# First feed-forward's second product as seven products of quarters, and a turn in written order on four queues

## The chip, the cores and the metric

The kernel runs on one core of a Trainium2 chip. The metric is the device time of one execution in microseconds (us). A core has five instruction queues that run beside one another, each in order: TensorE (PE in the profile; its weight loads are listed apart as PEld), VectorE (DVE), ScalarE (ACT), GpSimd (POOL) and SyncE (SP), which here only issues DMA transfers. All data is float32.

## The reference

Two graph layers act on 64 graphs of 256 nodes with 256 features. The first is a pair of graph attentions followed by a feed-forward; the second is a relational attention with eight heads followed by another feed-forward. Cut to what is computed:

```python
# layer 0
h = gat(gat(x, adj, W1, a1), adj, W2, a2)        # softmax over axis 1 of masked leaky_relu scores
h = layernorm(x + h)
ff = relu(h @ w_ff1 + b_ff1) @ w_ff2 + b_ff2     # 256 -> 1024 -> 256
x = layernorm(h + ff)
# layer 1
q, k, v_r = x @ Wq, x @ Wk, x @ Wv[r]            # r = 0..3
out = sum_r (softmax(q k^T / sqrt(32)) * (adj == r)) @ v_r
x = layernorm(x + out @ Wo)
return layernorm(x + gelu(x @ W1 + b1) @ W2 + b2)
```

`adj` holds only 0 and 1, and the kernel keeps the values of r = 0 and the difference of r = 1 to it. The product that the change is about is `... @ w_ff2` of the first feed-forward: 256 nodes by 1024 hidden units by 256 features for each graph.

## The kernel before

Graphs are handled two at a time: a unit has 512 nodes (`TN`), in four blocks of 128 (`T`), and there are 32 units. After a prologue that folds weights (`folding`) and brings the first two units under way, the loop runs `turn(y_, x_, z)` for `y_` = 0 to 31, with `x_ = y_ + 1` and `z = y_ + 2`. In one turn, three units are at different depths: Y goes through layer 1 from queries to the second feed-forward, X through the first feed-forward of layer 0, and Z through both graph attentions. In the last two turns Z, then X, are missing. A unit whose last norm is still to come is held in `waiting` and is finished in the next turn.

The order of work: within a `tc.manual_schedule(engines=...)` block the named queues issue exactly in the order of the program text; the other queues are ordered by a planner that goes by the costs it assumes. The whole loop lies in such a block for TensorE and SP. A second block inside `turn` adds VectorE and ScalarE, from `masks(0)` to `early_adjacency(z)`, that is, for the attention part of the turn. Behind it VectorE and ScalarE are ordered by the planner, and `behind(...)` queues some of their instructions behind named ones. GpSimd is the planner's throughout.

Names and lines that matter here:

- `hidden_seven` (products at L837, VectorE accumulation at L849, ScalarE copies and activations at L846, L855, L880, the differences of inputs at L820) computes a hidden layer, 256 to 1024, from seven products of quarters. A step such as `6a` is one product of one half; a step `r` or `s` is an activation. Products 1, 6, 7 and 4 of a half add up in one PSUM bank, and each waits until VectorE has read the sum before it. It is called twice in a turn, for X (`first`) and for Y (`second`).
- `hidden_out` (matmuls at L902, residual add at L906) is the first feed-forward's second product in the plain form: four node blocks, eight blocks of hidden units, 256 output columns each.
- `hidden_out_seven` (sums of quarters at L915 to L918, matmuls at L923, adds at L928) is the second feed-forward's second product from seven products of quarters; a product is eight matmuls of 128 output columns. `out_pieces` hands it out product by product.
- `gat_softmax` with its scores, leaky ReLU (L738), exponential (L739) and masks with row sums (L741), and `scaled_rows` (L750); `gat_first` (`hpp`, L759) is the first graph attention's product with the values, and `second_sums` (`ygp`, L770) the second's.
- `norm` (statistics on VectorE at L787 and L788, the power on GpSimd at L789 and L790), `applied_norm` (L797 on VectorE, L800 on ScalarE) and `affine` (L805, L806 on VectorE).
- `normed_features` transposes 32x32 blocks on VectorE (L667), then moves quadrants with four GpSimd copies and twelve DMAs (L676, L684, L686). Y's features before the second hidden layer go half over SP's queue and half over ScalarE's.
- `queries_keys` (L969 on TensorE, L971 on ScalarE), `values` (L982, L984), `weighted` (scores L998, exponentials L1004), `masked` (L1009), `node_sums` (L1014), `applied` (L1024, L1027), `divided` (L1035 to L1040), `add_blocks` (L770, L773).

PSUM has six rotating banks under the tag `g` and one each for `po` and `zo`.

Of the kernel before, what the change touches and what calls it, by code (L numbers as in the profile page):

```python
# [385 lines left out]
def narrow_path(  # L386
# [214 lines left out]
    wf1s, w1s, w2s = [], [], []  # L601

    def folding():
# [5 lines left out]
        wf1s.extend(seven(wf1, "wf1"))  # L609
        yield  # L610
# [116 lines left out]
    def gat_softmax(u, l, wh, rows, c, aT):  # L727

        name = f"{u}_{l}"
        s = (work.tile([P, T, N], F32, tag="s", name=f"s{name}", bufs=1) if u > 1 else  # L730
             work.tile([P, 2 * T, N], F32, tag="e", name=f"s{name}")[:, :T])
        z = work.tile([P, T], F32, tag="z", name=f"z{name}")
        for b in range(G):
            for t in range(b * NB, (b + 1) * NB):
                nc.scalar.activation(s[:, t, :], rows[:, b * N:(b + 1) * N], AF.Identity,
                                     bias=wh[:, t, c:c + 1])
            sb = s[:, b * NB:(b + 1) * NB, :].rearrange("p t n -> p (t n)")
            nc.vector.scalar_tensor_tensor(sb, sb, ALPHA, sb, op0=ALU.mult, op1=ALU.max)  # L738
            nc.scalar.activation(sb, sb, AF.Exp)  # L739
            for t in range(b * NB, (b + 1) * NB):  # L740
                nc.vector.scalar_tensor_tensor(s[:, t, :], s[:, t, :], 1.0, aT[:, t, :],  # L741
                                               op0=ALU.mult, op1=ALU.mult,
                                               accum_out=z[:, t:t + 1])
        nc.vector.reciprocal(z, z)
        nc.gpsimd.tensor_add(lowg, lowg, z)
        return s, z

    def scaled_rows(wh, z, w):
        for t in range(T):
            mark["scaled"] = nc.scalar.activation(wh[:, t, :w], wh[:, t, :w], AF.Copy, scale=z[:, t:t + 1])  # L750
# [28 lines left out]
    def norm(u, l, y, blocks=range(T)):  # L779
        n, t0 = f"{u}_{l}_{blocks[0]}", blocks[0]  # L780
        bt = slice(t0, t0 + len(blocks))
        st = work.tile([P, T, 6], F32, tag="st", name=f"st{n}")
# [12 lines left out]
    def applied_norm(y, blocks, mv, rs, nm):  # L795
        bt = slice(blocks[0], blocks[0] + len(blocks))
        nc.vector.scalar_tensor_tensor(nm[:, bt], mv[:, bt, 0], -1.0, rs[:, bt],  # L797
                                       op0=ALU.mult, op1=ALU.mult)
        for t in blocks:
            mark["normed"] = nc.scalar.activation(y[:, t, :], y[:, t, :], AF.Identity,  # L800
                                                  bias=nm[:, t:t + 1], scale=rs[:, t:t + 1])

    def affine(y, g_, b_):

        nc.vector.tensor_mul(y, y, g_[:, None, :].to_broadcast(list(y.shape)))  # L805
        nc.vector.tensor_add(y, y, b_[:, None, :].to_broadcast(list(y.shape)))  # L806

    def hidden_seven(u, l, hT, w, bi, func, h1, tt):
# [20 lines left out]
        def out(h, o, b):  # L829

            f = o * FB // 2 + 2 * h
            return h1[:, f:f + 2, b * N:(b + 1) * N]
# [18 lines left out]
        def done(h, o, b, ps=None):  # L851
            for i in range(2):
                f = o * FB // 2 + 2 * h + i
                y = h1[:, f, b * N:(b + 1) * N]
# [3 lines left out]
        def step(name):  # L858
# [19 lines left out]
            elif n == "r":  # L878
                for f in range(2 * h, 2 * h + 2):
                    nc.scalar.activation(h1[:, f, :], h1[:, f, :], func, bias=bi[:, f:f + 1])  # L880
# [15 lines left out]
    def hidden_out_block(u, l, y, h1, wo_, t):  # L896
        b, i = divmod(t, NB)
        if i == 0:
            hidden_ps[u, l] = bank(f"yfp{l}_{u}_{b}")
        ps = hidden_ps[u, l]  # L900
        for k in range(FB):
            nc.tensor.matmul(ps[:, i * F:(i + 1) * F], h1[:, k, t * P:(t + 1) * P], wo_[:, k, :],  # L902
                             start=(k == 0), stop=(k == FB - 1))
        if i == NB - 1:
            yb = y[:, b * NB:(b + 1) * NB, :].rearrange("p t f -> p (t f)")
            nc.vector.tensor_tensor(yb, ps, yb, ALU.add)  # L906

    def hidden_out_seven(u, l, y, h1, w, s1, s2, s3, s4):


        b11, b21, b22, t1, t2, t3, t4 = w
        K2, F2 = FB // 2, F // 2
        a11, a12, a21, a22 = (h1[:, k * K2:(k + 1) * K2, b * N:(b + 1) * N]
                              for b in range(2) for k in range(2))
        nc.vector.tensor_tensor(s1, a21, a22, ALU.add)  # L915
        nc.vector.tensor_tensor(s2, s1, a11, ALU.subtract)
        nc.vector.tensor_tensor(s4, a12, s2, ALU.subtract)
        mark["quarters"] = nc.vector.tensor_tensor(s3, a11, a21, ALU.subtract)  # L918

        def product(ps, a, w_, first):  # L920
            for i in range(NB):
                for k in range(K2):
                    nc.tensor.matmul(ps[:, i * F2:(i + 1) * F2], a[:, k, i * P:(i + 1) * P], w_[:, k, :],  # L923
                                     start=first and i == 0 and k == 0, stop=True, skip_group_check=True)

        def added(b, o, ps):
            yq = y[:, b * NB:(b + 1) * NB, o * F2:(o + 1) * F2]
            nc.vector.tensor_tensor(yq, ps[:, :F].rearrange("p (i f) -> p i f", i=NB), yq, ALU.add)  # L928

        n = f"{l}_{u}"  # L930
        one = bank(f"yf1{n}")
        product(one, a11, b11, True)
        added(0, 0, one)
        yield
        two = bank(f"yf3{n}")
        product(two, s1, t1, True)
        added(1, 1, two)
        yield
        ps = bank(f"yf2{n}")
        product(ps, a12, b21, True)  # L940
        added(0, 0, ps)
        yield
        product(one, s2, t2, False)
        added(0, 1, one)
        yield
        product(two, s4, b22, False)
        added(0, 1, two)
        yield
        product(one, s3, t3, False)
        added(1, 1, one)  # L950
        yield
        product(one, a22, t4, False)
        added(1, 0, one)
        yield

    hidden_ps = {}

    def hidden_out(u, l, y, h1, wo_):
        for t in range(T):
            hidden_out_block(u, l, y, h1, wo_, t)  # L960

    def queries_keys(u, hT):
        qk = []
        for w, c, name in ((wq, bq, "q"), (wk, bk, "k")):
            d = work.tile([P, KB, TN], F32, tag=name, name=f"{name}{u}", bufs=1)
            for m in range(KB):
                ps = bank(f"{name}p{u}_{m}")
                for k in range(KB):
                    nc.tensor.matmul(ps, w[:, k, m * P:(m + 1) * P], hT[k],  # L969
                                     start=(k == 0), stop=(k == KB - 1))  # L970
                nc.scalar.activation(d[:, m, :], ps, AF.Identity, bias=c[:, m:m + 1])  # L971
            qk.append(d)
        return qk
# [56 lines left out]
    def divided(u, b, po, zo, oT):  # L1030


        rz = work.tile([P, KB * N], F32, tag="rz", name=f"rz{u}_{b}", bufs=1)
# [27 lines left out]
    def first_rows(z):  # L1061
# [80 lines left out]
    def turn(y_, x_, z):  # L1142
# [132 lines left out]
        if Z:  # L1275
            second_rows(z)
# [105 lines left out]
```

## Time and profile before

| What | us |
|---|---|
| Median of three runs | 3129.61 (3126.61 to 3130.61) |
| The profiled execution | 3128.14 |
| Its span, first to last instruction | 3126.4 |
| L902, 64 matmul records, in one turn | 13.81 |
| L923, 16 matmul records | 1.78 |
| One steady turn, 1501.50 to 1596.24 | 94.74 |

The profile is of one execution, so its rows are to be set against 3128.14 and not against the median. The page gives each engine's busy time; a steady turn is cut into stretches to see which engine is busy where, and the order in time of each engine shows what an instruction waited for. A float32 matmul of this kernel leaves two records, each with a weight load; matmuls overlap at their ends, so the time of a row of them is taken from its start to the start of the next. A wait is shown in square brackets with the engine and line that ended it. TensorE's granted clock was 0.993 on average and full in the steady turns.

```profile
L902 PE MATMUL yfp<-wf,h 128*128 128x256 f32 x2048 | 447.3, 379 | 0.0
L1009 DVE TENSOR_TENSOR ea<-e,aT 128x1024 f32<-128x1024 f32 x256 | 313.2, 1253 | 79.7 <-ACT e L1004 79.7
L849 DVE TENSOR_TENSOR h<-h1a,h 128x512 f32<-128x512 f32 x384 | 263.9, 687 | 130.8 <-PE h1a L837 93.7
L787 DVE BATCH_NORM_STATS2 st<-y 128x6 f32<-128x256 f32 x512 | 198.1, 408 | 2.4
```

These rows are four of the costliest groups of instructions: line, engine, operation, tiles and shapes, count, then busy us, mean ns of one, and the idle time before them with what ended it.

### The profile page before, as it was taken

To read this page: it belongs to the slowest core of one execution; us is meant where nothing else is said; L and a number is where in the kernel's file an instruction comes from. 1 tells how busy PE (TensorE), PEld (TensorE's weight loads), DVE (VectorE), ACT (ScalarE), POOL (GpSimd) and SP (SyncE) were. 2 spreads that over 40 slices of the span, in tenths; PEclk is the share of its full clock that TensorE was granted. 3 is DMA by queue.
4 is the path that set the end of the run, shared out by engine and by line. 5 is a ranking of instruction groups with operands and counts; after the bars stand their busy time and mean duration, and the time that the engine had idled before them with its cause. 6 is when DMAs were issued, how large, how long until landed. Compare 5 with 4: busy or idle time off the path is not lost. (4 is left out here: it accounts for less than half of the span.)

```text
span 3126.4 us, 52820 instructions
## 1 busy us (share of the span) xinstructions
PE 3067.8 (98%) x19888; PEld 2327.7 (74%) x19888; DVE 2383.2 (76%) x4600; ACT 1626.6 (52%) x3274; POOL 602.5 (19%) x826
## 2 busy tenths in 40 slices
PE   7999999999999999999999999999999999999997
PEld 6677777778777778777777777787777787777766
DVE  4577777877877777777777778778778777778776
ACT  4355545555545555545555455555455555455543
POOL 3122111121111221121221111211111211212200
PEclk8999999999999999999999999999999999999999
DMA  5011111111011211111211111210111111211000
GB/s 147 13 36 34 20 38 38 43 41 33 19 42 38 43 36 24 32 43 38 43 34 20 38 38 43 43 31 20 41 38 43 36 31 25 43 38 36 22 13 15
DMA packets 428549, 113.55 MB, mean 36 GB/s; under 512 B 364760, under 2 KB 427648, under 8 KB 428288
## 3 DMA queue, kind: packets, MB, share of 16 engines
q1 hardware_dynamic: 417952, 102.66, 15.0%
q10 hardware_dynamic: 9280, 6.39, 0.8%
q8 instruction: 160, 2.62, 0.4%
q0 software_dynamic: 1056, 1.05, 0.1%
q14 instruction: 101, 0.83, 0.1%
HBM read 57.04 MB, written 16.78 MB: 24 GB/s over the span
## 5 line engine op out<-in xcount | busy, mean ns | idle before, releaser
L902 PE MATMUL yfp<-wf,h 128*128 128x256 f32 x2048 | 447.3, 379 | 0.0
L902 PEld LDWEIGHTS yfp<-wf,h 128*128 128x128 f32 x2048 | 386.8, 190 | 51.3
L1004 ACT ACTIVATE e<-sp 128x512 f32<-128x512 f32 x512 | 264.3, 603 | 282.4 <-PE sp L998 271.7
L846 ACT COPY h<-h1b 128x512 f32<-128x512 f32 x384 | 221.2, 584 | 333.9 <-PE h1b L837 331.5
L800 ACT ACTIVATE y<-y,nm,rs 128x256 f32<-128x256 f32 x512 | 270.1, 596 | 219.7 <-DVE nm L797 215.4
L1009 DVE TENSOR_TENSOR ea<-e,aT 128x1024 f32<-128x1024 f32 x256 | 313.2, 1253 | 79.7 <-ACT e L1004 79.7
L849 DVE TENSOR_TENSOR h<-h1a,h 128x512 f32<-128x512 f32 x384 | 263.9, 687 | 130.8 <-PE h1a L837 93.7
L684 POOL COPY hT<-yt 32x256 f32<-32x256 f32 x248 | 240.3, 969 | 215.9 <-DVE yt L667 187.9
L789 POOL TENSOR_SCALAR rs<-mv 128x4 f32<-128x4 f32 (+1 forms) x130 | 55.6, 428 | 1074.6 <-DVE mv L788 1069.0
L982 PE MATMUL vp<-wv,hT 128*128 128x512 f32 x480 | 214.0, 599 | 0.0
L787 DVE BATCH_NORM_STATS2 st<-y 128x6 f32<-128x256 f32 x512 | 198.1, 408 | 2.4
L676 POOL COPY hT<-yt 32x256 f32<-32x256 f32 x120 | 111.0, 925 | 392.3 <-DVE yt L667 388.6
L982 PEld LDWEIGHTS vp<-wv,hT 128*128 128x128 f32 x480 | 88.7, 190 | 110.4 <-issue 103.2
L880 ACT ACTIVATE h<-h,cols 128x512 f32<-128x512 f32 x256 | 167.5, 718 | 1.5 <-DVE h L849 1.1
L667 DVE STREAM_TRANSPOSE yt<-y 128x256 f32<-128x256 f32 x368 | 148.1, 428 | 25.0 <-ACT y L800 20.0
L806 DVE TENSOR_TENSOR y<-y,rb 128x1024 f32<-128x1024 f32 (+1 forms) x130 | 160.1, 1232 | 2.2
L805 DVE TENSOR_TENSOR y<-y,rg 128x1024 f32<-128x1024 f32 (+1 forms) x130 | 157.2, 1210 | 5.0 <-ACT y L800 2.3
L1014 DVE TENSOR_TENSOR es<-e 128x1024 f32<-128x1024 f32 x128 | 155.6, 1216 | 0.0
L998 PE MATMUL sp<-q,k 32*128 32x256 f32 x2048 | 147.3, 400 | 6.8 <-ACT k L971 5.0
L998 PEld LDWEIGHTS sp<-q,k 32*128 32x128 f32 x2048 | 92.7, 184 | 81.5 <-issue 46.3
L971 ACT ACTIVATE q<-qp,cols 128x512 f32<-128x512 f32 x64 | 43.4, 678 | 206.8 <-PE qp L969 206.8
L1024 PE MATMUL po<-e,v 128*32 128x256 f32 x2048 | 137.0, 385 | 0.0
(236 smaller groups left out, 6248.2 us busy)
## 6 DMA issues: line engine op xcount, KB each, us to landing
hT<-yt SPq DMA_DIRECT2D x918, 32.0 KB, 2.0
y<-in_x_dram SPq DMA_DIRECT2D x32, 512.0 KB, 5.3
xq<-in_x_dram SPq DMA_DIRECT2D x240, 64.0 KB, 2.2
aq<-in_adj_dram SPq DMA_DIRECT2D x240, 64.0 KB, 2.4
out_dram<-y SPq DMA_DIRECT2D x30, 512.0 KB, 3.1
hT<-yt ACTq DMA_DIRECT2D x186, 32.0 KB, 1.9
wf<-in_L_gnn_w_ff_dram SPq DMA_DIRECT2D x2, 1024.0 KB, 7.4
w<-in_L_gnn_W_dram SPq DMA_DIRECT2D x2, 1024.0 KB
```

The source lines that it names most:

```text
L684: nc.gpsimd.tensor_copy(to, at)
L787: nc.vector.bn_stats(st[:, t, :], y[:, t, :])
L800: mark["normed"] = nc.scalar.activation(y[:, t, :], y[:, t, :], AF.Identity, bias=nm[:, t:t + 1], scale=rs[:, t:t + 1])
L806: nc.vector.tensor_add(y, y, b_[:, None, :].to_broadcast(list(y.shape)))
L846: mark["copied"] = nc.scalar.copy(out(h, o, b), pair(ps))
L849: mark["added"] = nc.vector.tensor_tensor(out(h, o, b), pair(one[h]), out(h, o, b), ALU.add)
L880: nc.scalar.activation(h1[:, f, :], h1[:, f, :], func, bias=bi[:, f:f + 1])
L902: nc.tensor.matmul(ps[:, i * F:(i + 1) * F], h1[:, k, t * P:(t + 1) * P], wo_[:, k, :], start=(k == 0), stop=(k == FB - 1))
L982: nc.tensor.matmul(ps, hT[k][:, t * P:(t + 1) * P], wvf[:, k, :], start=(k == 0), stop=(k == KB - 1))
L998: nc.tensor.matmul(ps[a][:, j * N:(j + 1) * N], k_[hp, m, j0:j0 + P], q[hp, m, b * N:(b + 1) * N], start=True, stop=True)
L1004: mark[f"exp{b * KB + m}"] = nc.scalar.activation(e[:, a, :], ps[a], AF.Exp, scale=isd)
L1009: nc.vector.tensor_tensor(ea[:, a:a + 2, :], e[:, a:a + 2, :], ab[:, None, :].to_broadcast([P, 2, NB * N]), ALU.mult)
```

## The change

The first feed-forward's second product takes the form that the second one has. `hidden_out`, `hidden_out_block` and `hidden_out_seven` go; a class `HiddenOut` serves both, with `sums`, `product` and `add` as separate calls, so that each can be put at its own place in the turn. The weight `wf2` is turned into its seven quarters in the prologue by `seven_out`, four GpSimd instructions of 128x512. The order of products becomes 1, 2, 5, 6, 3, 7, 4 in the first feed-forward and 1, 5, 2, 6, 3, 7, 4 in the second.

The block in written order now spans the whole turn, from the queries to the last product, on TensorE, SP, VectorE and ScalarE (in the last turn on TensorE and SP). The calls of `behind` inside the turn are gone. `gat_softmax` becomes a class `Softmax` whose scores, exponentials and masks are placed one by one; `affine` is split into `times` and `plus`; two of the four blocks of X's second norm are applied by GpSimd. Several steps move: the features and norm of X from the end of the turn before to this turn's head, the last norm's statistics of the waiting unit there too, Z's first softmax and `first_sums` (`hpp`) to between the new products, `sums(2)` behind `4b`. The statistics tile has one buffer, and the tile `rz` shares a buffer with the softmax's `s`.

The diff, cut to its core: unchanged lines between the parts are left out, and of the old second half of `turn`, which is printed above, the removed lines too.

```diff
+        wf2s.extend(seven_out(wf2, "wf2"))
...
+    class Softmax:
+
+        def __init__(s, u, l, wh, rows, c):
+            s.u, s.wh, s.rows, s.c = u, wh, rows, c
+            s.s = (work.tile([P, T, N], F32, tag="s", name=f"s{u}_{l}", bufs=1) if u > 1 else
+                   work.tile([P, 2 * T, N], F32, tag="e", name=f"s{u}_{l}")[:, :T])
+            s.z = work.tile([P, T], F32, tag="z", name=f"z{u}_{l}")
+
+        def block(s, b):
+            return s.s[:, b * NB:(b + 1) * NB, :].rearrange("p t n -> p (t n)")
+
+        def scores(s, b):
             for t in range(b * NB, (b + 1) * NB):
-                nc.scalar.activation(s[:, t, :], rows[:, b * N:(b + 1) * N], AF.Identity,
-                                     bias=wh[:, t, c:c + 1])
-            sb = s[:, b * NB:(b + 1) * NB, :].rearrange("p t n -> p (t n)")
-            nc.vector.scalar_tensor_tensor(sb, sb, ALPHA, sb, op0=ALU.mult, op1=ALU.max)
-            nc.scalar.activation(sb, sb, AF.Exp)
+                nc.scalar.activation(s.s[:, t, :], s.rows[:, b * N:(b + 1) * N], AF.Identity,
+                                     bias=s.wh[:, t, s.c:s.c + 1])
+            nc.vector.scalar_tensor_tensor(s.block(b), s.block(b), ALPHA, s.block(b), op0=ALU.mult, op1=ALU.max)
+
+        def exp(s, b):
+            nc.scalar.activation(s.block(b), s.block(b), AF.Exp)
+
+        def masks(s, b):
             for t in range(b * NB, (b + 1) * NB):
-                nc.vector.scalar_tensor_tensor(s[:, t, :], s[:, t, :], 1.0, aT[:, t, :],
-                                               op0=ALU.mult, op1=ALU.mult,
-                                               accum_out=z[:, t:t + 1])
-        nc.vector.reciprocal(z, z)
-        nc.gpsimd.tensor_add(lowg, lowg, z)
-        return s, z
-
-    def scaled_rows(wh, z, w):
-        for t in range(T):
-            mark["scaled"] = nc.scalar.activation(wh[:, t, :w], wh[:, t, :w], AF.Copy, scale=z[:, t:t + 1])
+                nc.vector.scalar_tensor_tensor(s.s[:, t, :], s.s[:, t, :], 1.0, g[s.u]["aT"][:, t, :],
+                                               op0=ALU.mult, op1=ALU.mult, accum_out=s.z[:, t:t + 1])
+
+        def shares(s):
+            nc.vector.reciprocal(s.z, s.z)
+            nc.gpsimd.tensor_add(lowg, lowg, s.z)
+
...
-    def applied_norm(y, blocks, mv, rs, nm):
+    def applied_norm(y, blocks, mv, rs, nm, part=None, gpsimd=False):
         bt = slice(blocks[0], blocks[0] + len(blocks))
-        nc.vector.scalar_tensor_tensor(nm[:, bt], mv[:, bt, 0], -1.0, rs[:, bt],
-                                       op0=ALU.mult, op1=ALU.mult)
-        for t in blocks:
+        if part is None or part[0] == blocks[0]:
+            nc.vector.scalar_tensor_tensor(nm[:, bt], mv[:, bt, 0], -1.0, rs[:, bt],
+                                           op0=ALU.mult, op1=ALU.mult)
+        for t in part or blocks:
+            if gpsimd:
+                nc.gpsimd.tensor_scalar(y[:, t, :], y[:, t, :], rs[:, t:t + 1], nm[:, t:t + 1],
+                                        op0=ALU.mult, op1=ALU.add)
+                continue
...
+    class HiddenOut:
+
+
+
+        def __init__(s, u, l, y, h1, w, sums):
+            K2 = FB // 2
+            s.n, s.y, s.w, s.s = f"{l}_{u}", y, w, sums
+            s.a = [h1[:, k * K2:(k + 1) * K2, b * N:(b + 1) * N] for b in range(2) for k in range(2)]
+            s.ps = {}
+
+        def sums(s, *which):
+            a11, a12, a21, a22 = s.a
+            s1, s2, s3, s4 = s.s
+            for n in which:
+                o, x_, y_, op = ((s1, a21, a22, ALU.add), (s2, s1, a11, ALU.subtract),
+                                 (s3, a11, a21, ALU.subtract), (s4, a12, s2, ALU.subtract))[n - 1]
+                mark["quarters"] = nc.vector.tensor_tensor(o, x_, y_, op)
+
+        def product(s, n):
+            b11, b21, b22, t1, t2, t3, t4 = s.w
+            K2, F2 = FB // 2, F // 2
+            if n in (1, 2, 5):
+                s.ps[n] = bank(f"yf{n}_{s.n}")
+            for old, new in ((1, 6), (6, 7), (7, 4), (5, 3)):
+                if n == new:
+                    s.ps[n] = s.ps[old]
+            a, w_ = {1: (s.a[0], b11), 2: (s.a[1], b21), 5: (s.s[0], t1), 6: (s.s[1], t2),
+                     3: (s.s[3], b22), 7: (s.s[2], t3), 4: (s.a[3], t4)}[n]
             for i in range(NB):
                 for k in range(K2):
+                    nc.tensor.matmul(s.ps[n][:, i * F2:(i + 1) * F2], a[:, k, i * P:(i + 1) * P], w_[:, k, :],
+                                     start=n in (1, 2, 5) and i == 0 and k == 0, stop=True,
+                                     skip_group_check=True)
+
+        def add(s, n):
+            b, o = {1: (0, 0), 2: (0, 0), 5: (1, 1), 6: (0, 1), 3: (0, 1), 7: (1, 1), 4: (1, 0)}[n]
+            F2 = F // 2
+            yq = s.y[:, b * NB:(b + 1) * NB, o * F2:(o + 1) * F2]
+            nc.vector.tensor_tensor(yq, s.ps[n][:, :F].rearrange("p (i f) -> p i f", i=NB), yq, ALU.add)
+
+        def __call__(s, *which):
+            for n in which:
+                s.product(n)
+                s.add(n)
+
...
+        order = tc.manual_schedule(engines={getattr(mybir.EngineType, n) for n in
+                                            ("PE", "SP", "DVE", "Activation")[:4 if X else 2]})
+        with order:
+            query(0)
+            query(1)
+            if X:
+                applied_norm(X["y"], *X.pop("n"))
+            last = norm(waiting[0][0], 3, waiting[0][1]) if waiting else None
+            key(0)
+            key(1)
+            if X:
+                X["hT"] = normed_features(x_, 0, X["y"])
+                times(X["y"], rg1)
+            scores(0)
+            if z + 1 < NG:
+                load_x(z + 1)
             masks(0)
             totals(0)
-            v = values(y_, hT, range(T))
+            v = values(y_, hT, range(0, T // 2))
+            if waiting:
+                applied_norm(waiting[0][1], *last)
+            v = values(y_, hT, range(T // 2, T), v)
             steps = first_hidden(x_) if X else None
             scores(1)
             if Z:
@@ -1206,109 +1222,147 @@
             masks(2, (2,))
             first("5b 7a 3b ra 6b")
             totals(2)
-            first("4a 7b")
+            first("4a 7b rb")
+            if X:
+                plus(X["y"], rb1)
             scores(3)
-            first("sa rb sb", 2)
+            first("sa sb", 2)
             masks(3)
             totals(3)
-            sums(2)
-            last = norm(waiting[0][0], 3, waiting[0][1]) if waiting else None
             if Z:
                 project(z, range(0, T // 2))
             first("4b")
+            sums(2)
             sums(3)
+            if X:
+                out = HiddenOut(x_, 0, X["y"], X["h1"], wf2s, out_sums(x_, 0))
+                out.sums(1, 2)
             shares(1)
             out_(0)
             piece()
             if Z:
                 project(z, range(T // 2, T))
+            if Z:
+                early_adjacency(z)
             out_(1)
             if Z:
-                first_rows(z)
+                first_scores(z)
+            n = norm(y_, 2, y)
+            if X:
+                out(1)
+            if Z:
+                Z["m"].scores(0)
+                Z["m"].scores(1)
+                Z["m"].exp(0)
+                Z["m"].exp(1)
+            if X:
+                out.sums(4)
+                out(2, 5)
+            applied_norm(y, *n)
+            if Z:
+                Z["m"].masks(0)
+                Z["m"].masks(1)
+                Z["m"].shares()
+                Z["m"].scaled(WH)
+            if X:
+                out(6)
+                hT = normed_features(y_, 2, y, queues=(nc.sync, nc.scalar))
+                out(3)
+                out.sums(3)
+            else:
+                piece()
+                hT = to_features(y, f"h3T{y_}")
+                hT = [h.rearrange("p (t a r) -> p t a r", t=T, r=32) for h in hT]
+                affine(y, rg3, rb3)
             if waiting:
-                applied_norm(waiting[0][1], *last)
-            normed(y_, 2, y)
+                affine(waiting[0][1], rg4, rb4)
+                stored(*waiting.pop(), slice(0, T))
+            if z + 1 < NG:
+                load_rows(z + 1)
             if Z:
-                early_adjacency(z)
+                first_sums(z, range(0, T // 2))
+            if X:
+                out(7)
+            if Z:
+                first_sums(z, range(T // 2, T))
+            if X:
+                out.product(4)
+            tt = work.tile([P, HPB, NB * N], F32, tag="e", name=f"tt{y_}_1")
+            second = hidden_seven(y_, 1, hT, w1s, b1, AF.Gelu, Y, tt.rearrange("p a n -> p (a n)"))
+            if X:
+                out.add(4)
+                n = norm(x_, 1, X["y"])
+            h1 = Y["h1"] = work.tile([P, FB, TN], F32, tag="h1", name=f"h1{y_}_1", bufs=1)
+            second("2a 1a 2b 1b")
+            for t, name in enumerate(("5a", "5b", "3a", "3b")):
+                second(name)
+                if X:
+                    applied_norm(X["y"], *n, [t], t > 1)
+                if X and t == 0:
+                    affine(y, rg3, rb3)
+            second("6a 6b ra rb 7a 7b")
+            if Z:
+                X["hT"] = normed_features(x_, 1, X["y"], natural=True)
+            second("sa sb 4a 4b")
+            if X and not Z:
+                X["hT"] = to_features(X["y"], f"h2T{x_}")
+            if y_ >= NG - 2:
+                pieces = out_pieces(y_, y, h1)
+                if X:
+                    left.append(pieces)
+                    affine(X["y"], rg2, rb2)
+                else:
+                    for _ in pieces:
+                        pass
+                return
+            second_scores(z)
+            out = HiddenOut(y_, 1, y, h1, w2s, out_sums(y_, 1))
+            out.product(1)
+            out.sums(1, 2)
+            Z["m"].scores(0)
+            out.add(1)
+            out.product(5)
+            Z["m"].scores(1)
+            Z["m"].exp(0)
+            Z["m"].exp(1)
+            out.add(5)
+            out.sums(4, 3)
+            out(2)
+            Z["m"].masks(0)
+            out(6)
+            Z["m"].masks(1)
+            Z["m"].shares()
+            Z["m"].scaled(F)
+            out(3)
+            affine(X["y"], rg2, rb2)
+            out(7)
             checked(z, Z["aq"])
+            if z + 1 < NG:
+                load_adjacency(z + 1)
+            second_sums(z)
+            Z["n"] = norm(z, 0, Z["y"])
+            out(4)
+            waiting.append((y_, y))
...
-        hidden_out(0, 0, g[0]["y"], g[0]["h1"], wf2)
+        first = HiddenOut(0, 0, g[0]["y"], g[0]["h1"], wf2s, out_sums(0, 0))
+        first.sums(1, 2, 4, 3)
+        first(1, 2, 5, 6, 3, 7, 4)
         normed(0, 1, g[0]["y"])
         second_sums(1)
+        g[1]["n"] = norm(1, 0, g[1]["y"])
```

## The prediction

> **What bounds the kernel now.** I read the page's busy rows first, then busy time by stretch of one steady turn, then the order in time on each engine in that turn (1501.5 to 1596.2 us).
>
> ```profile
> PE 3067.8 (98%) x19888; PEld 2327.7 (74%) x19888; DVE 2383.2 (76%) x4600; ACT 1626.6 (52%) x3274; POOL 602.5 (19%) x826
> ```
> ```profile
> 1582.43:1596.24 13.81, 13.81 (x66) 12.16 (x65) 11.28 (x27) 6.14 (x13) 4.74 (x6) 1.00 0.12 30
> 1596.24:1611.89 15.65, 15.65 (x73) 13.46 (x72) 11.64 (x30) 12.83 (x27) 1.48 (x3) 1.00 0.00 0
> 1517.15:1534.00 16.85, 16.66 (x133) 16.05 (x132) 13.82 (x31) 8.54 (x18) 3.91 (x5) 1.00 0.31 48
> 1534.00:1582.43 48.43, 48.27 (x351) 30.13 (x349) 37.50 (x59) 23.10 (x46) 8.26 (x11) 1.00 0.18 45
> ```
>
> The second fence's columns are stretch, its length, then busy us of PE, weight loads, DVE, ACT, POOL, the clock and DMA. The four stretches are a whole turn, taken from two neighbouring ones: the product to be replaced, the second hidden layer, the second layer's output products, and attention. They add to 94.74 us; PE is busy in 94.38, DVE in 74.25. The clock is full. So PE sets the end, and only two things count: PE work that goes, and places where PE waits for an in-order neighbour. The waits are seen only in the order in time:
>
> ```profile
> 1517.59 1.95 PE L923 MATMUL yf<-w,h 128*128 128x128 f32 x16
> 1519.37 1.95 PE L923 MATMUL yf<-w2t,eq 128*128 128x128 f32 x16
> 1521.16 1.95 PE L923 MATMUL yf<-w,h 128*128 128x128 f32 x16
> 1523.30 2.05 PE L923 MATMUL yf<-w2t,eq 128*128 128x128 f32 x16 [0.19 <-DVE y L928]
> 1525.19 3.74 PE L923 MATMUL yf<-w,eaq 128*128 128x128 f32 x32
> ...
> 1537.44 3.60 PE L969 MATMUL kp<-hT,wk 128*128 128x512 f32 x8
> 1541.20 1.15 PE L998 MATMUL sp<-q,k 32*128 32x256 f32 x16 [0.17 <-ACT k L971]
> ...
> 1582.43 13.98 PE L902 MATMUL yfp<-wf,h 128*128 128x256 f32 x64
> 1596.24 1.03 PE L837 MATMUL h1b<-hT,w 128*128 128x256 f32 x4
> ```
>
> Columns: start, duration (ends overlap the next row, so I use start to start), instruction, wait. L902 is the replaced product. L923 is the same seven-product form, already running in the second feed-forward: the nearest possible row.
>
> **The product.** L902: 64 records from 1582.43 to 1596.24, 13.81 us. The new form has 7 x 8 matmuls of two records: 112 records of 128 columns. L923 runs 16 of them in 1.785 us (1517.59 to 1519.37 to 1521.16; 32 in 3.57), so seven products take 12.50. **Gain 1.31 us a turn.** A rule speaks against this: the Trainium skill, "TensorE: Matmul & The Clock Gate", section "Back-to-back issue gap", says that in a stream of weight load and matmul pairs the spacing does not fall in proportion to the columns, about 81 ns at 128 columns where the column count alone gives 56. A record here is two such passes (111.5 ns in the row, twice 56), so 81 ns would make 112 x 162 = 18.1 us: 4.3 us a turn lost, some 130 in all. In the row the weights load beside the matmuls; I take the row.
>
> **VectorE's new load.** Four sums of 128x1024 (1.19 to 1.40 us by L915 to L918) and seven adds of 128x256 (0.40, L928) come, two adds of 128x512 (0.68, L906) go: +6.5 us a turn, 74.25 to some 81 of 94. It still fits; what matters is where, for it now runs in written order. In the stretch after the attention output, PE's order is score rows 0.44, products 1, 2, 5, 6, 3, two first-graph sums (1.74), product 7, the other two (1.74), product 4. PE reaches product 7 at 0.44 + 8.93 + 1.74 = 11.1 us after the last `yop` matmul. Product 7 needs s3, and VectorE has in front of it, by start-to-start steps of the trace:
>
> ```profile
> 1582.19 0.69 DVE L773 TENSOR_TENSOR y<-yop,y 128x512 f32<-128x512 f32 x1 [2.30 <-PE yop L770]
> ...
> 1595.09 1.42 DVE L738 SCALAR_TENSOR_TENSOR s<-s 128x512 f32<-128x512 f32 x2 [0.78 <-ACT s L735]
> 1596.42 0.42 DVE L820 TENSOR_TENSOR tt<-hT 128x256 f32<-128x256 f32 x1
> ```
>
> start 0.17, residual add 0.61, statistics 4 x 0.53 = 2.11, add 1 0.34, leaky ReLU 1.33 (above), s4 1.13, adds 2 and 5 0.68, nm 0.08, masks and reciprocal 1.47, add 6 0.34, four transposes 1.96, add 3 0.34, s3 1.34: 11.9 us. All of it is ready in time (product 5 ends at 6.0, ScalarE's normalisation at 8.7). So product 7 starts at 12.0 instead of 11.1, plus 0.1 of restart as after 1523.30 (1.89 us for 16). **Cost 1.0.** Here the second rule: "SBUF — State Buffer", "Who interferes with whom", says that VectorE with two SBUF inputs and a GpSimd op reading SBUF lock each other out for a whole instruction. s3 falls beside the four GpSimd copies of hT (0.87 each). By the lock it could wait 0.87 more, and the turn would be almost level. The trace has L918 beside such copies at 1.42 against 1.22 in the last turns without: I take 1.34, already above.
>
> After that nothing more is late: affine of the waiting turn to 14.4, add 7, product 4 from 15.5; Y's hT. Turn 30 shows transposes done at 3009.2 and hT landed at 3014.7, 5.5 later: here 10.3 + 5.5 = 15.8, and the hidden layer starts at 17.3. That margin is 1.5 us. ScalarE's six DMA issues (3.73 us) now stand before the copies of hp; the rows that read hp come 12 us later.
>
> **The hidden layer without cover.** The two groups of hpp sums leave the second hidden layer. They stood between its last products, whose accumulation waits for VectorE. With them, 1508.49 to 1517.15 is 8.66 us less 3.48 of hpp, 5.18. Turn 30 has none:
>
> ```profile
> 3022.63 1.89 PE L837 MATMUL h1a<-tt,w1s 128*128 128x256 f32 x8
> 3024.51 3.91 PE L837 MATMUL h1a<-tt,w 128*128 128x256 f32 x16
> 3028.25 1.04 PE L652 MATMUL h2T31p<-ident,y 128*128 128x128 f32 x8
> ```
>
> 5.62 us. **Cost 0.44.** The moved affine (2.3 us) ends before the first of these adds is due.
>
> **Waits that go.** In the second layer, sums 1 and 2 are followed at once by adds 1 and 5, so product 6 no longer waits: 1525.19 - 1521.16 - 3.57 = **0.46 gained**. Next late there is the row scaling before ygp, done some 0.5 us ahead by the same addition. At the turn's head, the normalisation of X now stands between q and k on ScalarE instead of after q's first half: k's first half is ready at about 7.0 and not 7.2, so of the 0.33 us (1541.20 - 1537.44 - 3.43) some **0.2 is gained**.
>
> **The rest at nothing.** The waiting turn's statistics (2.1 us) go to the head, the bias half of affine (1.14) behind the first hidden layer: VectorE idles 0.41 before L1009 there, and values need its adds only 7 us later. X's transposes end about 0.6 later, its 12 DMAs (7.55 us on SP, and load_x's eight behind them) land near 16.3; the subtractions ran at 16.1 and the products at 18.7. If that cover were gone, each 1 us late is 1 us. sums(2) moves behind 4b: the same PE work; the projection now ahead of it needs a bank that comes free with the first exponential of scores(3), 0.1 either way. Store and load_rows stand behind six hT DMAs and before twelve due 10 us later; a store that lands slowly (3.1 us) stays inside. Two of four normalisations to GpSimd: no row has this shape; by L599's 128x256 tensor_scalar 0.46 to 0.70 each, by its adds 1.0; the transposes come 4 us later, either is covered. The folding adds four GpSimd ops of 1.26 to 2.2 us at 48 us, where GpSimd idled 5.5.
>
> **Sum.** A full turn: -1.31 - 0.46 - 0.2 + 1.0 + 0.44 = -0.53; 30 of these -16. The prologue's product -1. Turn 30, without hpp and softmax, gains 1.3 and loses about as much waiting for s3. Together -17. The profiled execution took 3128.1 (span 3126.4, 1.7 around it): 3111; the median is 1.5 above: **3112**.
>
> **Rivals.** (1) The cover holds: VectorE gets to s3 by 11.1, or the hidden layer's gap closes. Without the first cost, -1.53 a turn: 3082; without both, 3068. For it: the DVE list is within 8% of fitting. Against: its steps are measured back to back. (2) VectorE becomes the bound: every us that its list of 11.9 grows goes straight onto PE before product 7, and the second layer has only 0.4 to 0.5 of slack. From 0.53 more a turn the kernel is slower; at 1.0 more (the port lock, or some 0.06 at each of 18 handed-over steps) +0.47 a turn, 3143. Against: VectorE's waits on signals already posted cost nothing visible in the trace. (3) Narrow matmuls load-bound: 3260; L923 excludes it.
>
> **Numbers.** Likeliest 0.52, own range 3098 to 3122; rival 1 0.28; rival 2 0.12; level 0.08. A difference under 0.2% (6 us) can't be told from none here: faster 0.83, same 0.09, slower 0.08. Range 3076 to 3131.
>
> **What would show it.** The yf product's first-layer records at 111 ns; a PE gap before product 7 of about 1 us naming DVE's s3; 5.6 us for the last three pairs of the second hidden layer; none before the second layer's product 6. Wrong if DVE reaches s3 earlier, if hT's DMAs gate the hidden layer, or if SP's order delays X's features.

## The result, and the profile after

| | before | after |
|---|---|---|
| Median of five runs | 3129.61 (3126.61 to 3132.10) | **3093.99** (3093.45 to 3096.72) |
| Profiled execution | 3128.14 | 3093.86 |
| Its span | 3126.4 | 3092.2 |
| Up to the first score rows of turn 0 | 159.67 | 153.97 |
| Mean of the 29 turns from there, us | 94.79 | 93.75 |
| The rest, from turn 29 on | 217.82 | 219.37 |

Times in us. The ratio is 0.989, 95% interval 0.9876 to 0.9904: 35.6 us faster. In the profiled pair 34.2 us are to be explained: 29 x 1.04 = 30.0 in the turns, 5.7 in the prologue, less 1.55 at the end. A turn is counted from one start of the first attention's score rows (`rows<-ident,xp`) to the next.

First the page: busy us (share of the span) and instructions of each engine, then rows of its list of groups.

```profile
PE 3040.4 (98%) x21424; PEld 2331.4 (75%) x21424; DVE 2582.8 (84%) x4888; ACT 1602.3 (52%) x3212; POOL 654.9 (21%) x892
...
L876 DVE TENSOR_TENSOR h<-h1a,h 128x512 f32<-128x512 f32 x384 | 262.5, 686 | 95.4 <-PE h1a L864 92.5
...
L961 DVE TENSOR_TENSOR y<-yf,y 128x256 f32<-128x256 f32 x448 | 182.2, 407 | 19.8 <-PE yf L953 19.4
```

VectorE carries 200 us more, TensorE 27 less. L876 is the hidden layers' accumulation, shown of before as L849: its own time is as it was, and the idle time before it fell from 130.8 to 95.4. L961 is the adds of both feed-forwards, 448 in all, where the kernel before had those of one (L928). TensorE is still busy in 98%, so only its work and its waits count. Next, the four stretches of a steady turn, with the columns as in the view of before: second hidden layer, the second layer's output products, attention, and the new product.

```profile
1483.77:1496.49 12.72, 12.72 (x58) 10.10 (x57) 10.16 (x22) 9.10 (x16) 4.21 (x4) 1.00 0.14 41
1496.49:1512.89 16.40, 16.40 (x133) 15.98 (x132) 15.68 (x31) 7.66 (x17) 3.94 (x5) 1.00 0.21 33
1512.89:1560.94 48.05, 48.05 (x350) 30.22 (x349) 39.51 (x62) 25.21 (x50) 5.63 (x11) 1.00 0.17 29
1560.94:1577.29 16.35, 16.25 (x130) 15.46 (x129) 15.03 (x39) 7.88 (x18) 6.03 (x7) 1.00 0.20 57
```

This turn is 93.52 us (the median is 93.53; before 94.75). VectorE is busy in 80.38 of it. PE has 0.10 us without work in the last stretch and none elsewhere, but a busy row also hides waits at a matmul's end, so the time is read from start to start. The order in time on TensorE, from the second hidden layer on:

```profile
1488.95 2.08 PE L864 MATMUL h1b<-hT,w1s 128*128 128x256 f32 x8
1490.87 1.89 PE L864 MATMUL h1a<-tt,w1s 128*128 128x256 f32 x8
...
1496.49 0.60 PE L724 MATMUL rows<-ident,hp 128*128 128x128 f32 x4
...
1500.51 1.95 PE L953 MATMUL yf<-w,h 128*128 128x128 f32 x16
1502.29 1.95 PE L953 MATMUL yf<-w2t,eq 128*128 128x128 f32 x16
...
1516.33 3.60 PE L979 MATMUL kp<-hT,wk 128*128 128x512 f32 x8
1519.85 0.50 PE L1008 MATMUL sp<-q,k 32*128 32x256 f32 x4
```

1490.87 to 1496.49, the last three pairs of products, is 5.62 us. Product 6 of the second layer (1502.29) follows product 2 in 1.78 us: its wait is gone. Keys to scores is 3.52 us (3.76 before). The same view where the new product runs:

```profile
1560.94 3.74 PE L953 MATMUL yf<-wf,h 128*128 128x128 f32 x32
1564.52 3.74 PE L953 MATMUL yf<-wf2t,eq 128*128 128x128 f32 x32
1568.09 1.95 PE L953 MATMUL yf<-wf,eaq 128*128 128x128 f32 x16
1569.88 1.91 PE L775 MATMUL hpp<-xp,s 128*128 128x258 f32 x8
1571.88 2.05 PE L953 MATMUL yf<-wf,eaq 128*128 128x128 f32 x16
1573.77 1.91 PE L775 MATMUL hpp<-xp,s 128*128 128x258 f32 x8
```

Two products in 3.58 and 3.57 us, one in 1.79: 111.6 ns a record. Product 7 starts 2.00 us after `hpp`, which takes 1.74, and itself takes 1.89. So 0.37 us are lost there. VectorE's order in time in that place, before product 7:

```profile
1568.82 1.41 DVE L668 STREAM_TRANSPOSE yt<-y 128x256 f32<-128x256 f32 x4
1570.16 0.39 DVE L961 TENSOR_TENSOR y<-yf,y 128x256 f32<-128x256 f32 x1
1570.46 1.36 DVE L939 TENSOR_TENSOR eaq<-h 128x1024 f32<-128x1024 f32 x1
1571.75 1.41 DVE L830 TENSOR_TENSOR y<-y,rg 128x1024 f32<-128x1024 f32 x1
```

The four transposes take 1.34 us (1568.82 to 1570.16) and s3 is done at 1571.8, 11.3 us after the last `yop` matmul.

### The profile page after: what moved, and what is told of

Same layout as the page of the kernel before. It is cut to its first block, busy times and chain, and to the rows that moved or that the text cites. A ratio compares the mean times of both kernels' runs of the same rounds, so it can differ in the third digit from the quotient of the medians.

```text
span 3092.2 us, 56427 instructions
## 1 busy us (share of the span) xinstructions
PE 3040.4 (98%) x21424; PEld 2331.4 (75%) x21424; DVE 2582.8 (84%) x4888; ACT 1602.3 (52%) x3212; POOL 654.9 (21%) x892
## 5 line engine op out<-in xcount | busy, mean ns | idle before, releaser
L821 ACT ACTIVATE y<-y,nm,rs 128x256 f32<-128x256 f32 x450 | 238.5, 591 | 228.4 <-DVE nm L814 224.0
L876 DVE TENSOR_TENSOR h<-h1a,h 128x512 f32<-128x512 f32 x384 | 262.5, 686 | 95.4 <-PE h1a L864 92.5
L1047 POOL TENSOR_TENSOR low<-low,rq 128x16 f32<-128x16 f32 x64 | 13.9, 216 | 1088.3 <-DVE rq L1046 1088.3
L685 POOL COPY hT<-yt 32x256 f32<-32x256 f32 x248 | 210.5, 849 | 64.3 <-DVE yt L668 56.6
L803 DVE BATCH_NORM_STATS2 st<-y 128x6 f32<-128x256 f32 x512 | 204.3, 401 | 0.3
L961 DVE TENSOR_TENSOR y<-yf,y 128x256 f32<-128x256 f32 x448 | 182.2, 407 | 19.8 <-PE yf L953 19.4
L805 POOL TENSOR_SCALAR rs<-mv 128x4 f32<-128x4 f32 (+1 forms) x130 | 30.3, 233 | 788.5 <-DVE mv L804 772.0
L833 DVE TENSOR_TENSOR y<-y,rb 128x1024 f32<-128x1024 f32 (+1 forms) x130 | 166.8, 1284 | 3.2
L677 POOL COPY hT<-yt 32x256 f32<-32x256 f32 x120 | 113.5, 946 | 166.6 <-DVE yt L668 162.8
L806 POOL TENSOR_TENSOR rs<-rs,mhalf 128x4 f32<-128x4 f32 (+1 forms) x130 | 142.6, 1097 | 7.9
L668 DVE STREAM_TRANSPOSE yt<-y 128x256 f32<-128x256 f32 x368 | 131.7, 414 | 7.5 <-ACT y L821 6.1
```

Of the source, the lines that this page charges most:

```text
L685: nc.gpsimd.tensor_copy(to, at)
L803: nc.vector.bn_stats(st[:, t, :], y[:, t, :])
L876: mark["added"] = nc.vector.tensor_tensor(out(h, o, b), pair(one[h]), out(h, o, b), ALU.add)
L961: nc.vector.tensor_tensor(yq, s.ps[n][:, :F].rearrange("p (i f) -> p i f", i=NB), yq, ALU.add)
```

## The experiments

Each was timed beside the kernel before, the last two kernels in a second session (medians of before 3130.8 and 3130.7 us, some 1.2 us above the one beside the changed kernel); intervals are 95%. Turns are of the profiled execution.

| Kernel | median us | ratio to before | mean turn | median turn |
|---|---|---|---|---|
| the changed kernel | 3093.99 | 0.9890 (0.9876 to 0.9904) | 93.75 | 93.53 |
| product in plain form | 3130.47 | 0.9999 (0.9991 to 1.0008) | 95.07 | 94.78 |
| s3 early | 3087.87 | 0.9865 (0.985 to 0.988) | 93.54 | 93.30 |
| s3 twice | 3128.53 | 0.9997 (0.9989 to 1.0006) | 94.87 | 94.86 |
| another hidden order | 3111.62 | 0.9943 (0.9929 to 0.9956) | 94.29 | 94.27 |
| s3 early, norm on GpSimd | **3075.28** | 0.9824 (0.981 to 0.9837) | 93.16 | 93.05 |
| s3 early, statistics first | 3103.13 | 0.9911 (0.9897 to 0.9924) | 94.01 | 94.00 |

**The product in plain form.** The changed kernel in its written order, with 64 records of 256 columns in place of the seven products; the folding of `wf2` goes too.

```diff
-                out = HiddenOut(x_, 0, X["y"], X["h1"], wf2s, out_sums(x_, 0))
+                out = PlainOut(x_, X["y"], X["h1"])
```

`PlainOut` computes one node block at each of the places of products 1, 5, 3 and 4, adds behind the second and the fourth, and has no sums.

> The first feed-forward's second product is put back to its plain form (64 records of 256 columns, no sums of quarters, two adds of 128x512), all else in the new written order. My theory, the product pays for itself: TensorE gets 1.31 us a turn back to do, and the 0.37 us wait before product 7 goes, so some 0.95 us a turn more, 3120 to 3124 us. Rival, the written order is what brings the gain and the product only breaks even under VectorE's new load: 3090 to 3100.

The order with the plain product in it is worth nothing, and my 7 to 11 us were wrong. The prologue's 6.6 us are there (153.03 instead of 159.67), and are given back in this execution, which took 2.6 us more than the median: the mean turn is 0.28 us longer than before (8 us in 29 turns), the end 3.6. An undisturbed turn is level (94.73 us; before 94.74): 0.45 us are gained in the second layer's output products and 0.38 in attention, 0.64 are lost in the second hidden layer and 0.18 at the product. From here to the changed kernel such a turn falls by 1.21 us: the product's own 1.31, less the wait of 0.37 before product 7, and 0.27 that this kernel loses by itself. That the mean falls by 1.32, the product's saving, is chance.

Six turns took 95.6 to 97.0 us. In the longest of them VectorE waits for the features hT of the second hidden layer:

```profile
740.98 0.43 DVE L846 TENSOR_TENSOR tt<-hT 128x256 f32<-128x256 f32 x1 [5.55 <-DMA hT<-yt]
```

TensorE's first product of that layer then waits 1.25 us, and product 3b 0.70. Part of this is the edit's own: the add behind the second node block stands in VectorE's queue for 3.35 us, ahead of the normalisation, so the transposes that feed hT start 9.8 us after the score rows and not 8.3. So this run does not measure the order free of such losses. The new product in the old order was not tried, and how much of it the old order would have let through stays open.

**s3 early.** Is the 0.37 us before product 7 the place of s3 in VectorE's queue?

```diff
+            if X:
+                out.sums(3)
             out_(1)
...
                 out(3)
-                out.sums(3)
```

> The sum s3 moves from behind VectorE's transposes to before the second attention output add, where VectorE idles 1.15 us. If the wait before product 7 is VectorE's list up to s3, it goes, 0.37 us a turn: about 3083 us, and the record gap before product 7 closes. If something else holds product 7 there (the copies of hpp, a bank), the gap stays and the time is 3094, or more because the add behind s3 is late.

6.1 us faster than the change, not 11. VectorE's order in time shows s3 in the idle time ahead of the residual add, which does not start later for it (0.20 us after the last `yop` matmul, as in the change):

```profile
1462.59 1.18 DVE L939 TENSOR_TENSOR eaq<-h 128x1024 f32<-128x1024 f32 x1
1463.81 0.69 DVE L789 TENSOR_TENSOR y<-yop,y 128x512 f32<-128x512 f32 x1
```

On TensorE `hpp` then takes 1.74 us, product 7 1.78, and nothing waits:

```profile
1472.98 1.91 PE L775 MATMUL hpp<-xp,s 128*128 128x258 f32 x8
1474.72 1.95 PE L953 MATMUL yf<-wf,eaq 128*128 128x128 f32 x16
1476.50 1.91 PE L775 MATMUL hpp<-xp,s 128*128 128x258 f32 x8
```

An undisturbed turn is now 93.16 us, the expected 0.37 less. But the mean fell by 0.22 only: turns of 93.4 to 94.9 us had become longer and more frequent. The hidden layer starts 0.37 us earlier, and the transfers that it reads do not. These turns are taken up below.

**s3 twice.** The dose: what does a microsecond more in this queue cost?

```diff
-                out.sums(3)
+                out.sums(3, 3)
```

> s3 is computed twice in a row at its place, so VectorE's list before product 7 grows by one sum of 128x1024, 1.2 to 1.4 us a turn, and nothing else. If TensorE waits for that list, nearly all of it goes onto the time: product 7 waits some 1.6 us instead of 0.37, 3128 to 3136 us, no faster than before the change. If the turn has slack behind it, less than 10 us.

34.5 us. TensorE's order in time:

```profile
1586.76 1.91 PE L775 MATMUL hpp<-xp,s 128*128 128x258 f32 x8
1590.09 2.05 PE L953 MATMUL yf<-wf,eaq 128*128 128x128 f32 x16 [1.43 <-DVE eaq L939]
```

The second s3 takes 1.36 us and the undisturbed turn grew by 1.33: the slope is 1 from the start, so there was no slack left in the changed kernel before product 7. And all turns but two took the same 94.85 to 94.87: with the longer wait at product 7, VectorE no longer waits for the transfers behind it.

**The long turns.** In the changed kernel 11 of 29 turns took 0.2 to 1.1 us more than 93.52. One of them in order of time, first VectorE, then ScalarE, then TensorE:

```profile
732.96 0.43 DVE L847 TENSOR_TENSOR tt<-hT 128x256 f32<-128x256 f32 x1 [2.18 <-DMA hT<-yt]
...
738.55 0.16 DVE L814 SCALAR_TENSOR_TENSOR nm<-mv,rs 128x4 f32<-128x4 f32 x1 [0.39 <-POOL rs L806]
```

```profile
738.75 0.60 ACT L821 ACTIVATE y<-y,nm,rs 128x256 f32<-128x256 f32 x1 [0.40 <-DVE nm L814]
739.26 0.56 ACT L873 COPY h<-h1b 128x512 f32<-128x512 f32 x1
```

```profile
738.43 1.10 PE L864 MATMUL h1b<-hT,w1s 128*128 128x256 f32 x4
739.88 1.13 PE L864 MATMUL h1b<-hT,w1s 128*128 128x256 f32 x4 [0.34 <-ACT h L873]
```

The transfers of hT landed late (the six on SP's queue 3.6 us after issue instead of the usual 1.9). VectorE's four subtractions wait for them; behind these in VectorE's queue stand the statistics of X's norm, behind these GpSimd's power, then nm. ScalarE waits for nm with X's normalisation (738.75), and the copy that product 3b needs stands behind that (739.26). TensorE's second half of that row waits for the copy. The first products of the layer, which read hT themselves, were in time. The other long turns fit: in all 11 the subtractions begin 16.1 to 16.8 us after the score rows, in the 18 others 15.2 to 16.0. Three kernels try this chain.

**Another hidden order**, tried on the change itself, moves products 5a and 5b forward, so that there is more room before 3b:

```diff
-            second("2a 1a 2b 1b")
-            for t, name in enumerate(("5a", "5b", "3a", "3b")):
+            second("2a 1a 5a 2b 1b 5b")
+            for t, name in enumerate(("3a", "6a", "3b", "6b")):
...
-            second("6a 6b ra rb 7a 7b")
+            second("ra rb 7a 7b")
```

> The second hidden layer's products go 2a 1a 5a 2b 1b 5b 3a 6a 3b 6b 7a 7b 4a 4b, so that two products instead of one stand between 5 and 3 and between 6a and 7a. My theory, these waits are latencies of VectorE's add and of ScalarE's copy between products of one bank: the 0.11 us before 3b (0.4 more in every third or fourth turn) and some 0.15 of the 0.44 of the last three pairs go, about 0.45 us a turn, near 3080. Rival, they are a cost of VectorE's total load and move elsewhere: 3090 to 3096.

A miss: 17.6 us slower than the change. The long turns are gone (none above 94.46), and the hidden layer takes 12.69 us where it took 12.72, so the 0.26 us hoped for inside it did not come either. Instead a new wait stands in every turn, on TensorE in the second layer's output products:

```profile
1502.63 0.60 PE L724 MATMUL rows<-ident,hp 128*128 128x128 f32 x4
...
1505.55 2.02 PE L953 MATMUL yf<-w2t,eq 128*128 128x128 f32 x16 [0.53 <-DVE eq L939]
```

ScalarE's last copy comes 8.1 us after the hidden layer's start instead of 7.3. Behind it stand the load of the gelu table (1.28 us) and the activations that the first sum reads, and product 5 starts 2.92 us after the score rows instead of 2.23. I had looked at TensorE's waits in this layer and not at what else stood behind the copies.

**The norm on GpSimd** takes X's normalisation out of ScalarE's queue, on top of the early s3:

```diff
-                    applied_norm(X["y"], *n, [t], t > 1)
+                    applied_norm(X["y"], *n, [t], True)
```

> The early s3 (3087.9 us) with all four blocks of X's second norm applied by GpSimd, so that no instruction that needs nm stands between ScalarE's copies of the second hidden layer. My theory: in the turns of the early-s3 run that took more than 93.16 us (mean 93.54), late DMAs of hT hold VectorE's subtractions, these the statistics, these nm, and nm the copies that product 3b waits for. Then the copies run free: the wait of 0.1 before 3b goes in every turn and most of the mean excess of 0.38 too; about 0.35 x 29 = 10 us less: 3076 to 3081. Rival: the late DMAs reach TensorE directly, at the first products that read hT or at 5a's subtracted input: 3085 to 3090. A second rival: four GpSimd applications of 1.48 us end 5.9 us after nm, so that VectorE's transposes and the second layer's first sum behind them come late: product 5 of the second layer waits, 3095 or more.

12.6 us faster than the early s3, as the first theory has it: mean excess over the shortest turn 0.11 us instead of 0.38, and the wait before 3b gone, as TensorE and GpSimd show:

```profile
1479.33 1.97 PE L864 MATMUL h1b<-hT,w1s 128*128 128x256 f32 x8
1481.13 1.89 PE L864 MATMUL h1a<-tt,w1s 128*128 128x256 f32 x8
```

```profile
1478.76 4.02 POOL L818 TENSOR_SCALAR y<-y,rs,nm 128x256 f32<-128x256 f32 x4 [0.30 <-DVE nm L814]
```

Products 3a and 3b now take 1.80 us (1479.33 to 1481.13), where the changed kernel had 1.92 (1488.95 to 1490.87). The transfers come late as often as before: the subtractions begin 16.1 us or more after the score rows in 11 of 29 turns here too, but these turns take 93.05 to 93.70 us. So the chain was cut, and not its cause. The rival has a small part: in two turns of the early s3 (94.74 and 94.88) TensorE's first product of the layer waits 0.4 and 1.0 us as well. In the profiled pair 11.0 us come from the turns; the end is 4.6 shorter, most of it by a higher granted clock in the last turn (22.8 us at 1.00 for what the early s3 did in 25.3 at 0.85). It is the fastest version, 0.9824 of before.

**Statistics first** attacks the chain at its other end, again on top of the early s3:

```diff
+            if X:
+                out.add(4)
+                n = norm(x_, 1, X["y"])
             tt = work.tile([P, HPB, NB * N], F32, tag="e", name=f"tt{y_}_1")
...
-            if X:
-                out.add(4)
-                n = norm(x_, 1, X["y"])
```

> The early s3 (3087.9 us) with VectorE's last add and the statistics of X's second norm ahead of the four subtractions for the second hidden layer. My theory (late hT reaches TensorE through VectorE's in-order subtractions, the statistics, nm and ScalarE): the statistics no longer stand behind the DMAs, nm is ready when the copies come, and the subtractions, first needed by 5a 3.5 us into the hidden layer, still have over 1 us to spare in a good turn: 3076 to 3082. Rival: the late DMAs reach TensorE directly: 3085 to 3090. A second rival: the subtractions, now about 2.3 us later and 1.7 us long, make the first accumulations (1a, 1b) or 5a late in every turn: 3095 or more.

15.3 us slower than the early s3, the second rival's side, though mostly by another place. The statistics end at 1489.3. VectorE, then TensorE, in order of time:

```profile
1489.48 0.43 DVE L847 TENSOR_TENSOR tt<-hT 128x256 f32<-128x256 f32 x1 [0.22 <-issue]
...
1490.97 1.28 DVE L876 TENSOR_TENSOR h<-h1a,h 128x512 f32<-128x512 f32 x2
1492.17 0.15 DVE L814 SCALAR_TENSOR_TENSOR nm<-mv,rs 128x4 f32<-128x4 f32 x1
```

```profile
1491.87 1.11 PE L864 MATMUL h1b<-hT,w1s 128*128 128x256 f32 x4
1493.47 1.13 PE L864 MATMUL h1b<-hT,w1s 128*128 128x256 f32 x4 [0.50 <-ACT h L873]
1494.44 1.89 PE L864 MATMUL h1a<-tt,w1s 128*128 128x256 f32 x8
```

All but one turn take 93.99 to 94.00 us: the late transfers do no harm any more, since the subtractions start later anyway. But nm, which was to come earlier, comes later: it still stands behind the first two accumulations (1490.97), these now behind the subtractions, and it starts 5.66 us into the layer instead of 4.36. The copy that 3b needs stands behind it on ScalarE: of the 0.84 us that the turn is longer, 0.65 are lost between 3a and 3b (0.50 of it shown as a wait in the last fence), the rest at the products 5a and 5b before them.

## Why the prediction was right, and where its size was wrong

The forecast was 17 us and the change gave 35; the direction, the limits of the range and most steps held, but 3094 lies below the 3098 to 3122 that were given as likeliest.

- **The product, -1.31.** Exact: 111.6 ns a record, and rival 3 is out. The loss of 4.3 that the prediction held against it read the Trainium skill ("TensorE: Matmul & The Clock Gate", "Back-to-back issue gap") as 81 ns for each of two passes in a record. But that figure is for a pair of weight load and matmul, and the trace has one weight load for each record (21424 of either on the page). Counted so, 81 ns lie below the 111.6 measured and limit nothing.
- **The wait before product 7, +1.0. This is the step that failed:** it measured 0.37. The list of VectorE up to s3 was put at 11.9 us and was 11.2. Two terms make 0.75 of the difference, and the others give 0.1 back: the four transposes, put at 1.96 and measured at 1.34, and the leaky ReLUs, 1.33 and 1.20. Both came from rows in which VectorE took its blocks from ScalarE one by one, so that they had ScalarE's pace in them: the transposes from a row of four behind a wait for ScalarE's normalisation (1.96 us to the next start), the ReLUs from the row quoted in the prediction. In the new order the operands lie ready. The trace of before had such a row too: three transposes in 1.06 us in the steady turn. VectorE in the kernel before, turn 30 and the steady turn:

```profile
3007.29 1.92 DVE L667 STREAM_TRANSPOSE yt<-y 128x256 f32<-128x256 f32 x4 [0.67 <-ACT y L800]
...
1587.87 1.06 DVE L667 STREAM_TRANSPOSE yt<-y 128x256 f32<-128x256 f32 x3
```

  0.63 us in 29 turns is 18 us, the distance between 3112 and 3094. The other deviations below, of both signs, cancel to within 2 us; that they do is luck. Since the cost is a difference of two sums of 11 us, an error of 6% in one of them decided more than half of it.
- **The hidden layer without cover, +0.44; product 6, -0.46; scores, -0.2.** 0.44, 0.46 and 0.24 in the trace.
- **What the sum lacked.** Product 3b waits 0.11 in every turn for ScalarE, the two groups of sums in attention save 0.14, and the long turns cost 0.22 on the mean. For the last the prediction had hT land 5.5 us after the transposes (5.7 in the trace) with a margin of 1.5 (1.4) before the hidden layer's first product, and had no term for a late hT. The margin at that product held; the loss came by a queue that I had not followed: the statistics behind the subtractions.
- **The prologue, -1:** 5.7. Before, the first queries waited twice for the copies of h2T. On TensorE, in order of time:

```profile
106.16 2.05 PE L969 MATMUL qp<-h2T,wq 128*128 128x512 f32 x2 [2.44 <-ACT h2T L653]
109.96 2.90 PE L969 MATMUL qp<-h2T,wq 128*128 128x512 f32 x3 [1.75 <-DVE h2T L653]
```

VectorE had unit 1's norm and transposes ahead of its copy. The change moves these into turn 0, and the queries run without a wait. I had counted only the product there. **Turn 30** was put at even and lost 0.86 (77.48 us instead of 76.62 from its queries to those of the last turn): without Z nothing lies between its products 3 and 7, and TensorE waits 1.65 us for s3. Turn 29's part of the end gains 0.85, so the 1.55 us by which the end is longer are the last turn's. Nearly all of it stands in one stretch there, with the same work at a lower granted clock (1.00 before, 0.87 after; the clock is the third figure from the right), for a reason that these traces do not show. Before, then after:

```profile
3062.35:3085.08 22.73, 18.56 (x178) 14.53 (x179) 15.37 (x37) 6.60 (x13) 3.61 (x9) 1.00 0.04 13
3026.61:3050.79 24.18, 20.80 (x179) 16.27 (x179) 15.54 (x37) 6.79 (x13) 3.61 (x9) 0.87 0.03 12
```

- **GpSimd's normalisation**, put at 0.46 to 1.0 us a block, took 1.48, and was covered.
- **The rivals.** The first, in its first half, is what the early s3 makes: 94.75 to 93.16 in an undisturbed turn, 1.59 less where 1.53 was worked out. The second is shown as a mechanism, not as the outcome: the slope is 1, and one more s3 puts the kernel level with the one before (0.9997), where 0.53 us more than 11.9 was named as that point. Measured, that list is 11.2 + 1.3 = 12.5.

With the measured terms: -1.31 + 0.37 + 0.44 - 0.46 - 0.24 + 0.11 - 0.14 + 0.22 = -1.01 a turn, against -1.04 in the trace; before, too, the mean lay 0.04 above the usual turn.

## What to carry to other kernels

A step's duration taken from an in-order queue can hold the pace of its partner: before adding such steps to a list, look in the trace for the same instruction with its operands ready. Where a cost is the small difference of two long lists, give it as a range from their error. When a queue gets a written order, follow each transfer's waiter to what stands behind it in that queue, and from there to the engine that counts: a late transfer here reached TensorE over VectorE, GpSimd and ScalarE, and one move of work to GpSimd, which had time, brought 12.6 us, a third of what the whole change gave.

## What was not expected of the hardware

- GpSimd's 128x256 normalisation takes 1.45 to 1.51 us a block when two run beside VectorE's affine, and 0.55 at the least in the kernel with four of them: there the four span 4.02 us together, so two of 1.5 and two of 0.55, and the affine, 2.7 us long, began 0.2 us before the first. The Trainium skill ("SBUF — State Buffer", "Who interferes with whom") has a VectorE instruction with two SBUF inputs and a GpSimd instruction that reads SBUF exclude each other. For GpSimd that fits: it began 0.2 us into a VectorE instruction of 1.22, and an estimate of 1.0 of waiting plus 0.55 is about 1.5. VectorE's own halves of the affine took 1.22 and 1.46. s3 beside GpSimd's copies took 1.36, and 1.18 in the early place where GpSimd idles, not a whole copy more.
- The twelve transfers of hT, 32 KB each, are slow in nearly all of the long turns and in hardly any other. The six on SP's queue land in 1.9 to 2.6 us (the median of a turn) in undisturbed turns and in up to 3.9 in long ones, and the issuing queues are slower as well (in the turn shown, six on ScalarE's in 4.8 us instead of 3.7). Between 8 and 18 us after the score rows the instruction queue q8 moved data in 10 of the 11 long turns of the changed kernel and in 6 of the 18 others. So the late transfers go with instruction fetches; that a fetch makes them late is not shown, and the cause stays open.
